# Graph attention on one Trainium2 core: first source terms in blocks of sixteen windows, and first-edge one-hots that are stored once and multiplied in bfloat16 parts

## The chip, the core and the metric

The kernel runs on one core of a Trainium2 chip. TensorE (PE, with PEld for its weight loads), VectorE (DVE), ScalarE (ACT) and GpSimd (POOL) each work through a queue of their own; SyncE (SP) issues most of the transfers, and POOL issues the gathers. The metric is the device time of one execution in microseconds; a lower time is better. Several runs of a kernel are made, and their median is given. One more execution is recorded by the hardware profiler, with its own time.

## The reference, cut to what matters

A graph of N = 6250 nodes with 128 features each and E = 100,000 edges, sorted by their target `dst`, goes through four sublayers, each as `x = x + layer(relu(layernorm(x)))`: a mean of neighbours with two weights, a filter with a product over each node's edges, three mean layers ("SAGE"), and three attention layers. The change concerns the attention layers and what is prepared for them:

```python
def gat_conv(x, src, dst, ea, W, a_src, a_dst, We, a_edge, bias):
    s, d = concat([src, loops]), concat([dst, loops])     # each node also has a loop to itself
    h = x @ W
    al_s, al_d = h @ a_src, h @ a_dst
    al_e = ea_full @ We @ a_edge
    alpha = leaky_relu(al_s[s] + al_d[d] + al_e, 0.2)
    ex = exp(alpha - segment_max(alpha, d)[d])
    coef = ex / (segment_sum(ex, d)[d] + 1e-16)
    return segment_sum(h[s] * coef[:, None], d) + bias
for l in (1, 2, 3):
    h = batch_norm(leaky_relu(gat_conv(h, ...), 0.01))
```

So an edge needs one number of its source (`al_s[s]`, the "source term"), one of its target (`al_d[d]`), and a softmax over all edges of the same target.

## The kernel before, in words

*Tiling.* Nodes lie on P = 125 partitions with T = 50 nodes each. The attention layers treat the nodes in two ways. The *early* nodes, those of the first 64 partitions, are aggregated by matrix products with one-hot matrices. The *late* nodes, 3050 of them as R2 = 122 partitions with T2 = 25 each, are aggregated by gathers and a running sum. The late edges lie as 125 partitions with C2 = 400 edges each, in the order of their targets.

*What is prepared once.* During the first SAGE layer, `late_edges` (L1118) computes for each late node `lt.q` and `lt.c`: the partition and the column of its first edge; `lt.slot` is a row of the numbers 0 to 399. `early_edges` (L1187) stores one-hots of the early edges in DRAM in bfloat16, among them `hot_t` (which source partition an edge has, 128 windows of 128 x 128 for each of GP = 5 groups) and `col` (which of the 50 nodes of that partition). A tile pool in `late_edges` has one buffer for each name (`bufs=1`). The scheduler puts this work among the first products of SAGE layer 0 (L848), whose operands (`piece`, L884) come from DRAM over SP's queue, as the new tiles of this case would.

*A layer* (`attention_split`, L1297) makes h, al_s and al_d with TensorE, stores h with al_s as a table (`gtable`) and al_d (`own_d`), reads al_d of the late nodes back as `late_d` [122, 25] and of the early nodes as `early_d`, and splits al_s into three bfloat16 parts whose sum is al_s (`parts`). Then `split_edges` (L1370) does the edges, and a batch normalization ends the layer. In `split_edges`:

- `source_terms(g, al_s)` (L1376) finds the source terms of one group of early edges. In each of 16 rounds it loads 8 windows of `hot_t` and `col`, does 24 matmuls into `x_ps` (8 windows by three parts, L1387), and on DVE multiplies by `col` (L1391, recorded as the helper's line L73) and sums (L1392).
- `softmax(g, al_s)` (L1395) is the softmax over one group, eight steps, mostly small DVE operations that follow one another.
- `ready(step)` (L1439) loads and builds the one-hots `hot_n` and `hot_c` for one of 160 steps of four windows; `product(unit, m)` (L1459) is the aggregation of a quarter of a group, 50 matmuls (L1464).
- `late()` (L1475) is the late work as a generator: 50 blocks of eight columns with four steps each. A block gathers eight rows for each partition with POOL (L55), computes exponentials and the running sum on DVE, and stores it. Then `late_fix` (L1599, 7 steps) and `late_tail` (L1635, 5 rounds of 8 steps) follow: the latter gathers each late node's last sum, loads its own row of the table (`own_h`, L1642) and finishes it.
- `first_edges()` (L1518) brings al_d to the late edges. For each of 25 columns of late nodes DVE builds a one-hot `run` [122, 125], scaled by `late_d` (L1524), and a one-hot `col_f` [122, 400] (L1525), and TensorE adds their fp32 product to `at_ps` (L1526). The result has al_d at each node's first edge; a scan (L1532) spreads it over the node's other edges, and it is added to `ade`, the edge term of the late edges. The first column comes by a gather instead (L1530).

*The order.* PE, DVE and ACT do their instructions of `split_edges` in the order of the program: a chain of dependencies is laid over them at the end (L1591 to 1597). SP's and POOL's order is the scheduler's. The program's order is this: first `source_terms(0)` with `first_edges` drawn into it, which is the *lead-in's* first part; then `softmax(0)`, with one step of late work after each of its steps; then the *loop* of 160 steps. A loop step does four fp32 matmuls (L1564), prepares step + 2, draws seven matmuls of the last unit's product, evicts to `m` (L1569), and does a part of the next group's source terms and softmax. The late work is drawn by a count: after step s, `10 + 1.3 (s + 1)` of its 200 block steps are to be done (L1577), and from step 149 on three steps of what follows are drawn in each loop step (L1580). What is left of it comes after the last product.

*Names that the change touches.* The buffers `m` (two, 125 x 50 x 160 fp32, one for each unit of eight loop steps) and `hot_n` (three, 128 x 1000 fp32), the PSUM buffers `cnt` (two, 1024 fp32 a partition) and `o` (two; `at_ps` takes one), the SBUF buffers `acc` (two) and `run` (two). A transfer over all 125 partitions goes through `bulk` (L48), which makes two of it, over 112 and 13 partitions.

Of the kernel before, what the change touches and what calls it, by code (L numbers as in the profile page):

```python
# [9 lines left out]
F32 = mybir.dt.float32  # L10
BF16 = mybir.dt.bfloat16
I32 = mybir.dt.int32
AF = mybir.ActivationFunctionType
OP = mybir.AluOpType
AX = mybir.AxisListType
# [4 lines left out]
P = 125  # L20
C = E // P
T = N // P
# [3 lines left out]
NW, NG, WCAP = 5, 10, 128  # L26
# [4 lines left out]
P1, C2 = 64, 400  # L31
N1, E1 = P1 * T, E - P * C2
R2, T2 = 122, 25
# [6 lines left out]
def kernel(ctx: ExitStack, tc: tile.TileContext, a: dict, out: bass.AP):  # L40
    nc = tc.nc

    const = ctx.enter_context(tc.tile_pool(name="const", bufs=1))
    dram = ctx.enter_context(tc.tile_pool(name="dram", bufs=1, space=DRAM))
# [9 lines left out]
    def gather(dst, table, idx):  # L54
        nc.gpsimd.indirect_dma_start(  # L55
            out=dst, out_offset=None, in_=table,
            in_offset=bass.IndirectOffsetOnAxis(ap=idx, axis=0))
# [14 lines left out]
    def tt(o, x, y, op):  # L72
        nc.vector.tensor_tensor(o, x, y, op)  # L73

    def ts(o, x, s1, op0, s2=None, op1=None):
        if op1 is None:
            nc.vector.tensor_scalar(o, x, s1, None, op0=op0)  # L77
        else:
            nc.vector.tensor_scalar(o, x, s1, s2, op0=op0, op1=op1)  # L79

    def stt(o, x, s, y, op0, op1):
        nc.vector.scalar_tensor_tensor(o, x, s, y, op0=op0, op1=op1)  # L82
# [957 lines left out]

    late_hist = dram.tile([P * C2 + 1, W], F32, name="late_hist")

    class Late:


# [72 lines left out]
    def late_edges(lt):  # L1118
        with tc.tile_pool(name="le", bufs=1) as pool, tc.tile_pool(name="le_ps", bufs=1, space=PSUM) as ps:
# [58 lines left out]
            ts(inside[:, 1:2], inside[:, 0:1], -SKIP, OP.mult, SKIP, OP.add)  # L1178
            ts(fse[:, 2:3], fse[:, 1:2], -float(E1), OP.add)
            stt(lt.fix, fse[:, 2:3], inside[:, 0:1], inside[:, 1:2], OP.mult, OP.add)  # L1180

            row_ps = ps.tile([128, P], F32, name="le_row")
            transpose(row_ps, dst_f[:, C2 - 1:C2].to_broadcast([P, 128]))
# [186 lines left out]
    def split_edges(lt, i, table, own_d, bias, parts, early_d, late_d, ade, tails, stats, stats_l, pool, ps):  # L1370
# [144 lines left out]
            yield from late_fix(lt, tails, pool, ps)  # L1515
            yield from late_tail(lt, table, late_d, lt.e_self[i], bias, stats_l, pool, ps)

        def first_edges():  # L1518

            at_ps = ps.tile([P, C2], F32, name="at_ps", tag="o", bufs=2)  # L1520
            for c in range(T2):
                run = pool.tile([R2, P], F32, name="run")
                col = pool.tile([R2, C2], F32, name="col_f")
                ts(run, lt.slot[:R2, :P], lt.q[:, c:c + 1], OP.is_equal, late_d[:, c:c + 1], OP.mult)  # L1524
                ts(col, lt.slot[:R2, :], lt.c[:, c:c + 1], OP.is_equal)  # L1525
                nc.tensor.matmul(at_ps, lhsT=run, rhs=col, start=(c == 0), stop=(c == T2 - 1))  # L1526
                yield
            at_start = pool.tile([P, C2], F32, name="at_start", bufs=1)
            nc.scalar.activation(at_start, at_ps, AF.Copy)
            gather(at_start[:, 0:1], own_d, lt.first)  # L1530
            yield
            nc.vector.tensor_tensor_scan(at_start, lt.same, at_start, 0.0, op0=OP.mult, op1=OP.add)  # L1532
            tt(ade, ade, at_start, OP.add)
            yield

        traced = nc.cur_bb.bb.instructions
        n0 = len(traced)
        steps = GP * 32
        al_s = pool.tile([128, 128], F32, name="al_s")
        edges_late, firsts = late(), first_edges()  # L1540
        for n, _ in enumerate(source_terms(0, al_s)):
            if n >= 4:
                next(firsts, None)
        for _ in firsts:
            pass
        for n, _ in enumerate(softmax(0, al_s)):
            next(edges_late)
        hots = [ready(0)]
        next(edges_late)
# [1 line left out]
        done = n + 2  # L1551
        before, m = iter(()), None
        for step in range(steps):
            g, s = divmod(step, 32)
            unit, u = divmod(step, 8)
            if s == 0 and g < GP - 1:
                al_s = pool.tile([128, 128], F32, name="al_s")
                terms, soft = source_terms(g + 1, al_s), softmax(g + 1, al_s)
            if u == 0:
                m = pool.tile([128, T, NW, 32], F32, name="m")  # L1560
            cnt = ps.tile([128, 4, 256], F32, name="cnt", bufs=2)
            hot_n, hot_c = hots.pop(0)
            for w in range(4):
                nc.tensor.matmul(cnt[:P, w, :T * NW], lhsT=hot_c[:, w, :P], rhs=hot_n[:, w, :], start=True, stop=True)  # L1564
            if step + 2 < steps:
                hots.append(ready(step + 2))
            for _ in islice(before, 7):
                pass
            nc.scalar.activation(m[:P, :, :, u * 4:u * 4 + 4].rearrange("p l k q -> p k l q"),  # L1569
                                 cnt[:P, :, :T * NW].rearrange("p w (k l) -> p k l w", k=NW), AF.Copy)  # L1570
            if g < GP - 1:
                if s < 20:
                    for _ in islice(terms, 2 if s % 5 < 3 else 1):
                        pass
                else:
                    next(soft, None)
            while done < min(200, 10 + (step + 1) * 1.3):  # L1577
                next(edges_late)
                done += 1
            if step > 148:  # L1580
                for _ in islice(edges_late, 3):
                    pass
            if u == 7:
                for _ in before:
                    pass
                before = product(unit, m)
# [410 lines left out]
```

## Time and profile before

| | |
|---|---|
| median of 3 runs | 7281.8 us (7275.46 to 7299.53) |
| profiled execution: its time, its span | 6198.65 us, 6196.9 us |
| mean granted TensorE clock | 0.854 |
| attention layer 0, 1, 2: first source term starts | 3713.16, 4531.79, 5354.40 us |
| their first loop matmul | 3818.95, 4637.62, 5461.27 us |
| their loop step 149 | 4410.8, 5232.8, 6055.7 us |
| their last product's matmuls start | 4476.35, 5299.11, 6121.13 us |
| their batch normalization starts | 4508.87, 5331.48, 6153.65 us |
| SAGE layers, with what is prepared for attention | from about 2190 to 3713 us |

The profiled execution took 1083 us less than the median of the runs. The profile is of that one execution; places in it are given in microseconds from the start of its span. A row of groups names a line, an engine, an operation, its output and inputs with their shapes and the number of such instructions, then their busy time, the mean duration of one in nanoseconds, and the idle time of the engine ahead of them with what ended it. Where a helper records the instruction the line is the helper's: L55 is a gather, L73, L77 and L82 are DVE operations. A row of a table of stretches gives busy time and count for PE, PEld, DVE, ACT and POOL, then the granted TensorE clock, the busy share of the 16 DMA engines and the gigabytes a second that they moved. A row of a timeline gives start, duration, engine, line and operation; "SPq" is SP's queue, and such a row is the issue of a transfer and not its landing.

The largest groups of an attention layer are, by the trace of layer 0 (3713 to 4532 us): the gathers of rows on POOL, 402.5 us in 400; the loop's fp32 matmuls (L1564), 309.1 us in 1280; the product's (L1464), 303.2 us in 2000; ACT's `hot_c` (L1455), 233.9 us in 640; the eviction to `m` (L1569), 157.9 us in 160; DVE's running sum (L82), 141.2 us in 399. The source terms' matmuls (L1387) take 73.2 us in 1921.

### The profile page before, as it was taken

To read this page: it belongs to the slowest core of one execution; us is meant where nothing else is said; L and a number is where in the kernel's file an instruction comes from. 1 tells how busy PE (TensorE), PEld (TensorE's weight loads), DVE (VectorE), ACT (ScalarE), POOL (GpSimd) and SP (SyncE) were. 2 spreads that over 40 slices of the span, in tenths; PEclk is the share of its full clock that TensorE was granted. 3 is DMA by queue.
4 is the path that set the end of the run, shared out by engine and by line. 5 is a ranking of instruction groups with operands and counts; after the bars stand their busy time and mean duration, and the time that the engine had idled before them with its cause. 6 is when DMAs were issued, how large, how long until landed. Compare 5 with 4: busy or idle time off the path is not lost. (4 is left out here: it accounts for less than half of the span.)

```text
span 6196.9 us, 99429 instructions
## 1 busy us (share of the span) xinstructions
PE 5145.0 (83%) x34443; PEld 3914.9 (63%) x34443; DVE 4012.7 (65%) x12892; ACT 3053.7 (49%) x6329; POOL 2222.9 (36%) x2177
## 2 busy tenths in 40 slices
PE   3299996898888579989979986999859998679995
PEld 3267763444444457756657764888738888468885
DVE  7899976999999541156552126777457775477773
ACT  0166657999999310000000012777627667357674
POOL 0100007777776400000000004666326665256661
PEclk9999995655555589989989987999969999789997
DMA  1133336666665146468875534766337665366662
GB/s 42 28 133 136 137 143 178 193 193 200 194 193 177 34 172 229 182 240 298 310 276 211 190 128 141 199 193 183 107 107 206 194 192 140 90 172 193 193 181 82
DMA packets 410722, 1051.98 MB, mean 170 GB/s; under 512 B 83516, under 2 KB 206429, under 8 KB 391909
## 3 DMA queue, kind: packets, MB, share of 16 engines
q1 hardware_dynamic: 334356, 899.22, 43.4%
q0 software_dynamic: 70080, 143.09, 10.1%
q8 instruction: 273, 4.47, 0.3%
q10 hardware_dynamic: 5768, 3.19, 0.2%
q14 instruction: 245, 2.01, 0.1%
HBM read 742.37 MB, written 302.92 MB: 169 GB/s over the span
## 5 line engine op out<-in xcount | busy, mean ns | idle before, releaser
L55 POOL DMA_INDIRECT rows<-gtable,l_src x1200 | 1210.4, 1009 | 1651.2 <-DMA hot_t<-hot_t 1003.5
L848 PEld LDWEIGHTS <-parts 128*128 128x128 bf16 x12000 | 1181.2, 98 | 449.6 <-issue 37.0
L848 PE MATMUL o<-piece,parts 128*128 128x305 bf16 (+1 forms) x9000 | 1249.8, 299 | 23.1 <-DMA piece<-adj 23.1
L1464 PE MATMUL o<-m,hst 125*128 125x160 f32 x6000 | 913.8, 304 | 98.2 <-ACT m L1569 98.2
L1464 PEld LDWEIGHTS o<-m,hst 125*128 125x128 f32 x6000 | 874.9, 193 | 140.9 <-ACT m L1569 121.4
L1564 PE MATMUL cnt<-hot_n,hot_c 128*125 128x250 f32 x3840 | 931.2, 385 | 15.3 <-ACT m L1569 9.8
L55 POOL DMA_INDIRECT rows<-table,src_all x800 | 817.0, 1021 | 256.1 <-issue 210.1
L1564 PEld LDWEIGHTS cnt<-hot_n,hot_c 128*125 128x125 f32 x3840 | 701.2, 191 | 94.0 <-ACT m L1569 13.1
L1455 ACT ACTIVATE hot_c<-hot,coef_t 128x125 f32<-128x125 bf16 x1920 | 701.6, 390 | 0.1
L865 ACT ACTIVATE h_t<-h_ps 128x500 f32<-128x500 f32 x80 | 34.6, 432 | 968.5 <-PE h_ps L863 761.7
L1569 ACT ACTIVATE m<-cnt 125x1000 f32<-125x1000 f32 x480 | 473.8, 987 | 34.1 <-PE cnt L1564 34.0
L816 ACT ACTIVATE adj<-cnt 128x1000 bf16<-128x1000 f32 x320 | 382.8, 1214 | 182.7 <-PE cnt L814 181.1
L661 PE MATMUL z<-w,s 128*125 128x128 f32 x1600 | 369.8, 402 | 113.8 <-DVE s L82 113.5
L848 PE MATMUL o<-adj,parts 128*128 128x320 bf16 (+1 forms) x3000 | 451.8, 297 | 9.4 <-ACT adj L816 8.7
L661 PEld LDWEIGHTS z<-w,s 128*125 128x125 f32 x1600 | 316.4, 293 | 219.9 <-DVE s L82 185.0
L82 DVE SCALAR_TENSOR_TENSOR acc<-acc,ex,rows 125x130 f32<-125x130 f32 x1197 | 423.1, 353 | 34.3
L1454 ACT ACTIVATE hot_n<-half_n 128x250 f32<-128x250 bf16 x960 | 384.0, 400 | 32.9 <-DMA half_n<-node 32.3
L652 PE MATMUL z<-bf,w 128*128 128x500 f32 x400 | 376.4, 1042 | 27.0 <-ACT bf L621 27.0
L850 DVE COPY agg<-o 128x320 f32<-128x320 f32 x80 | 38.5, 482 | 521.6 <-PE o L848 521.6
L73 DVE TENSOR_TENSOR one<-x_ps,col 128x400 f32<-128x400 f32 x240 | 137.3, 572 | 360.0 <-PE x_ps L1387 301.3
L77 DVE TENSOR_SCALAR hot_n<-slots_b,id_t 128x250 bf16<-128x250 bf16 x1250 | 359.9, 288 | 0.0
L77 DVE TENSOR_SCALAR hot_p<-slots_b,hi_t 128x128 bf16<-128x128 bf16 x1250 | 316.7, 253 | 37.3 <-PE cnt L814 37.2
(463 smaller groups left out, 7167.6 us busy)
## 6 DMA issues: line engine op xcount, KB each, us to landing
piece<-adj SPq DMA_DIRECT2D x60, 2000.0 KB
piece<-adj SPq DMA_DIRECT2D x60, 1906.2 KB
late_hist<-acc SPq DMA_DIRECT2D x150, 455.0 KB
hot_t<-hot_t SPq DMA_DIRECT2D x240, 256.0 KB
hot<-hot SPq DMA_DIRECT2D x240, 256.0 KB
half_n<-node SPq DMA_DIRECT2D x480, 125.0 KB
dist<-ew_dram SPq DMA_DIRECT2D x50, 1000.0 KB
ea<-in_edge_attr SPq DMA_DIRECT2D x100, 448.0 KB
```

Source lines behind the costliest of these rows:

```text
L55: nc.gpsimd.indirect_dma_start(out=dst, out_offset=None, in_=table, in_offset=bass.IndirectOffsetOnAxis(ap=idx, axis=0))
L77: nc.vector.tensor_scalar(o, x, s1, None, op0=op0)
L82: nc.vector.scalar_tensor_tensor(o, x, s, y, op0=op0, op1=op1)
L652: nc.tensor.matmul(z1, lhsT=w1, rhs=bf, start=False, stop=True)
L661: nc.tensor.matmul(z2[:, j, :], lhsT=s1[:, j, :], rhs=w2, start=False, stop=j == HB - 1)
L816: nc.scalar.activation(adj[:, :, :, q - q0:q - q0 + n], cnt[:, :n, :T * NW].rearrange("p w (k l) -> p k l w", k=NW), AF.Copy)
L848: yield nc.tensor.matmul(o[:, :n], lhsT=parts[:, l, s, :], rhs=adj(l), start=(l == 0 and s == 0), stop=(l == T - 1 and s == 2))
L1454: nc.scalar.activation(hot_n[:, w, :], half_n[:, w // 2, :], AF.Copy)
L1455: nc.scalar.activation(hot_c[:, w, :P], lt.hot[:, w0 % WB + w, :P], AF.Copy, scale=coef_t[g][:, w0 + w:w0 + w + 1])
L1464: nc.tensor.matmul(o, lhsT=hst[:, l, :D], rhs=m[:P, l, :], start=(l == 0), stop=(l == T - 1))
L1564: nc.tensor.matmul(cnt[:P, w, :T * NW], lhsT=hot_c[:, w, :P], rhs=hot_n[:, w, :], start=True, stop=True)
L1569: nc.scalar.activation(m[:P, :, :, u * 4:u * 4 + 4].rearrange("p l k q -> p k l q"), cnt[:P, :, :T * NW].rearrange("p w (k l) -> p k l w", ...
```

## The change: what it does

There are four parts.

1. *One-hots stored once.* `late_edges` also builds all 25 one-hots of `run` (128 wide, not scaled) and of `col_f` (400 wide) in bfloat16, five columns at a time, and stores them in two DRAM tensors, `run_dram` [122, 3200] and `first_dram` [122, 10000]: 50 DVE operations and ten stores, in all 3.2 MB.
2. *`first_terms` in place of `first_edges` and of `source_terms(0)`.* At a layer's start two transfers bring `hot_t` of group 0, 64 windows each, and two bring `col`, into the two buffers `m`; one brings all of `run`, behind the first half. Five transfers bring the first-edge one-hots, five columns each, into the three `hot_n` buffers. The source terms run as 8 blocks of 16 windows in a `cnt` buffer (48 matmuls, then one multiplication and one sum of 800 elements a partition). `late_d` is split into three bfloat16 parts after block 1. After each of blocks 2 to 6, five columns of first edges are done: ACT scales the stored `run` by each of the three parts (`late_p`), and TensorE adds the three bfloat16 products to `at_ps`. The other groups keep `source_terms` as it is.
3. *Order.* `softmax(0)`'s first three steps are drawn between the parts of `first_terms`, so that five and not eight of them have a late step after them. The gather of the first column goes to a tile of its own, `at_first`, ahead of everything else in `split_edges`.
4. *Pace of the late work.* `10 + 1.45 (s + 1)` in place of `10 + 1.3 (s + 1)`, and three steps of the rest from step 141 on in place of 149.

```diff
+    run_dram = dram.tile([R2, T2 * 128], BF16, name="run1")
+    first_dram = dram.tile([R2, T2 * C2], BF16, name="first1")
+    KC = 5
...
+            for c0 in range(0, T2, KC):
+                runs = pool.tile([R2, KC, 128], BF16, name="le_runs")
+                cols = pool.tile([R2, KC, C2], BF16, name="le_cols")
+                for c in range(KC):
+                    ts(runs[:, c, :], lt.slot[:R2, :128], lt.q[:, c0 + c:c0 + c + 1], OP.is_equal)
+                    ts(cols[:, c, :], lt.slot[:R2, :], lt.c[:, c0 + c:c0 + c + 1], OP.is_equal)
+                nc.sync.dma_start(run_dram[:, c0 * 128:(c0 + KC) * 128], runs.rearrange("p c j -> p (c j)"))
+                nc.sync.dma_start(first_dram[:, c0 * C2:(c0 + KC) * C2], cols.rearrange("p c j -> p (c j)"))
...
-        def first_edges():
...
-            for c in range(T2):
-                run = pool.tile([R2, P], F32, name="run")
-                col = pool.tile([R2, C2], F32, name="col_f")
-                ts(run, lt.slot[:R2, :P], lt.q[:, c:c + 1], OP.is_equal, late_d[:, c:c + 1], OP.mult)
-                ts(col, lt.slot[:R2, :], lt.c[:, c:c + 1], OP.is_equal)
-                nc.tensor.matmul(at_ps, lhsT=run, rhs=col, start=(c == 0), stop=(c == T2 - 1))
-                yield
+        def first_terms(al_s):
+            XB, HW = 16, 64
+            stores = []
+            for h in range(2):
+                m = pool.tile([128, T, NW, 32], F32, name="m").rearrange("p l k q -> p (l k q)").bitcast(BF16)
+                hot_t, col = m[:, :HW * 128], m[:, HW * 128:HW * (128 + T)]
+                nc.sync.dma_start(hot_t, hot_t_dram[0][:, h * HW * 128:(h + 1) * HW * 128])
+                nc.sync.dma_start(col, col_dram[0][:, h * HW * T:(h + 1) * HW * T])
+                stores.append((m, hot_t.rearrange("p (w j) -> p w j", j=128), col.rearrange("p (w l) -> p w l", l=T)))
+                if h == 0:
+                    runs = m[:R2, HW * (128 + T):HW * (128 + T) + T2 * 128]
+                    nc.sync.dma_start(runs, run_dram)
+            cols = []
             at_ps = ps.tile([P, C2], F32, name="at_ps", tag="o", bufs=2)
+            def columns(k):
+                col = pool.tile([128, 4, T * NW], F32, name="hot_n", bufs=3)
+                col = col.rearrange("p w n -> p (w n)").bitcast(BF16)[:R2, :KC * C2]
+                nc.sync.dma_start(col, first_dram[:, k * KC * C2:(k + 1) * KC * C2])
+                return col
...
+            def late_parts():
+                for k in range(3):
+                    nc.vector.tensor_copy(late_b[:, k % 2, :], late_d if k == 0 else late_p[:, 2, :])
+                    nc.vector.tensor_copy(late_p[:, k, :], late_b[:, k % 2, :])
+                    if k < 2:
+                        tt(late_p[:, 2, :], late_d if k == 0 else late_p[:, 2, :], late_b[:, k % 2, :], OP.subtract)
+            def first_edge(c):
+                if c % KC == 0:
+                    cols.append(columns(c // KC))
+                run = pool.tile([R2, 3, 128], BF16, name="run", bufs=3)
+                for k in range(3):
+                    nc.scalar.activation(run[:, k, :P], runs[:, c * 128:c * 128 + P], AF.Copy, scale=late_p[:, k, c:c + 1])
+                for k in range(3):
+                    nc.tensor.matmul(at_ps, lhsT=run[:, k, :P], rhs=cols[-1][:, c % KC * C2:(c % KC + 1) * C2],
+                                     start=(c == 0 and k == 0), stop=(c == T2 - 1 and k == 2))
+            c = 0
+            for b in range(8):
+                _, hot_t, col = stores[b // 4]
+                w0 = b % 4 * XB
+                x = ps.tile([128, 4, 256], F32, name="cnt", bufs=2).rearrange("p a b -> p (a b)").rearrange(
+                    "p (h n) -> p h n", h=2)[:, :, :8 * T].rearrange("p h (w l) -> p h w l", l=T)
+                for w in range(XB):
+                    for k in range(3):
+                        nc.tensor.matmul(x[:, w // 8, w % 8, :], lhsT=hot_t[:, w0 + w, :], rhs=parts[:, k, :],
+                                         start=(k == 0), stop=(k == 2))
+                one = pool.tile([128, 2, 8, T], F32, name="acc")
+                tt(one, x, col[:, w0:w0 + XB, :].rearrange("p (h w) l -> p h w l", h=2), OP.mult)
+                nc.vector.tensor_reduce(al_s[:, b * XB:(b + 1) * XB].rearrange("p (h w) -> p h w", h=2), one, AX.X, OP.add)
+                if b == 1:
+                    late_parts()
+                while 2 <= b and c < min(T2, (b - 1) * 5):
+                    first_edge(c)
+                    c += 1
+                if b == 5:
+                    yield
             at_start = pool.tile([P, C2], F32, name="at_start", bufs=1)
-            nc.scalar.activation(at_start, at_ps, AF.Copy)
-            gather(at_start[:, 0:1], own_d, lt.first)
+            nc.scalar.activation(at_start[:, 1:], at_ps[:, 1:], AF.Copy)
+            nc.scalar.activation(at_start[:, 0:1], at_first, AF.Copy)
             yield
             nc.vector.tensor_tensor_scan(at_start, lt.same, at_start, 0.0, op0=OP.mult, op1=OP.add)
             tt(ade, ade, at_start, OP.add)
...
-        edges_late, firsts = late(), first_edges()
-        for n, _ in enumerate(source_terms(0, al_s)):
-            if n >= 4:
-                next(firsts, None)
-        for _ in firsts:
-            pass
-        for n, _ in enumerate(softmax(0, al_s)):
+        at_first = pool.tile([P, 1], F32, name="at_first", bufs=1)
+        gather(at_first, own_d, lt.first)
+        edges_late, soft = late(), softmax(0, al_s)
+        terms = first_terms(al_s)
+        next(terms)
+        next(soft)
+        next(terms)
+        next(soft)
+        next(soft)
+        next(terms, None)
+        for n, _ in enumerate(soft):
             next(edges_late)
...
-            while done < min(200, 10 + (step + 1) * 1.3):
+            while done < min(200, 10 + (step + 1) * 1.45):
...
-            if step > 148:
+            if step > 140:
```

## The prediction

> **What bounds the kernel now.** I read the page first, then the busy time by stretch of attention layer 0, the groups of its first stretch, the timelines of three places, and the DMA queues of one short window.
>
> ```profile
> PE 5145.0 (83%) x34443; PEld 3914.9 (63%) x34443; DVE 4012.7 (65%) x12892; ACT 3053.7 (49%) x6329; POOL 2222.9 (36%) x2177
> PEclk9999995655555589989989987999969999789997
> ```
>
> TensorE has the largest share, but that is an average. The change lies in the three attention layers (3713 to 6155 us), so each is cut where its work changes. Columns: stretch, length, busy time of PE, PEld, DVE, ACT, POOL, granted clock, DMA share, GB/s.
>
> ```profile
> 3713.10:3797.60 84.50, 51.49 (x434) 30.04 (x434) 35.60 (x89) 1.79 (x2) 24.16 (x25) 0.61 0.38 109
> 3797.60:3819.00 21.40, 0.99 (x3) 0.41 (x3) 19.96 (x62) 1.84 (x8) 9.16 (x9) 0.50 0.24 64
> 3819.00:4410.80 591.80, 554.60 (x4499) 512.97 (x4500) 435.40 (x1287) 431.07 (x1192) 370.43 (x368) 0.98 0.68 192
> 4410.80:4476.30 65.50, 44.06 (x246) 38.57 (x244) 22.15 (x95) 38.71 (x102) 22.94 (x24) 0.90 0.24 64
> 4476.30:4508.90 32.60, 17.64 (x110) 15.29 (x110) 12.83 (x55) 9.45 (x24) 3.49 (x4) 0.74 0.05 10
> ```
>
> In order: first source terms with first edges; first softmax; the loop to step 149; the loop with the late tail; the last product and the rest of the late tail. No engine is full in the first stretch, and the clock is 0.61. The second is DVE's. The third is TensorE's. The lead-in, from the first source term to the loop's first matmul, takes 105.8, 105.8 and 106.9 us in the three layers. Its largest groups:
>
> ```profile
> L1526 PE MATMUL at_ps<-col_f,run 122*125 122x400 f32 x50 | 38.5, 871 | 22.5 <-DVE col_f L77 22.5
> L1387 PE MATMUL x_ps<-als_parts,hot_t 128*128 128x50 bf16 x384 | 19.9, 209 | 6.6 <-DMA hot_t<-hot_t 3.6 <-DVE one L73 1.3 <-DMA gtable<-hst 1.1
> L73 DVE TENSOR_TENSOR one<-x_ps,col 128x400 f32<-128x400 f32 x16 | 9.2, 575 | 42.9 <-PE x_ps L1387 39.2 <-issue 3.7
> ```
>
> PE and DVE wait for each other in turn: this is what the blocks of 16 and the stored one-hots take away. The line that decides, I think, is elsewhere. own_h (L1642) is the only sizeable load in the kernel over 122 partitions in one DMA; a window in which it runs alone:
>
> ```profile
> DMA packets 84, 0.22 MB, mean 44 GB/s; under 512 B 0, under 2 KB 0, under 8 KB 84
> q1 hardware_dynamic: 84, 0.22, 12.8%
> ```
>
> 12.8% of 16 engines is two engines, at 44 GB/s, where 2 MB piece loads show 311 GB/s (2700 to 3100 us).
>
> **What the skill says.** "DMA: Bandwidth & Descriptors", section "Why a DMA increments its semaphore by 16 and not by 1": a transfer takes the largest number of engines, up to 16, that divides the slowest dimension on both sides, always the lowest-numbered ones; 122 has no such divisor but 2. The trace agrees (12.8%). The same page, "Queues, rings and completion order": each engine takes a queue's descriptors in order, so a transfer on all 16 waits behind one that sits on two. No run here shows that yet. "TensorE: Matmul & The Clock Gate", Part 1: the clock halves after idle windows; the trace agrees (0.50 to 0.61 in the lead-in, 0.98 in the loop).
>
> **The change, part by part.**
>
> *Loads of the lead-in.* Per layer SP now issues, after the ald stores: col (0.8 MB), late_d, early_d, runs (122 rows of 6,400 B), the second hot_t (2.1 MB), col, and three of five first-edge blocks (122 rows of 4,000 B), the last two as hot_n buffers come free. Only the first hot_t goes ahead of the table stores. An own_h row of 2,600 B costs two engines 2600/22 = 118 ns. [...]4,000 B cost about 0.17 us and 6,400 B 0.26 us. Each engine then has 61 x 0.26 = 15.6 us for runs, 5 x 61 x 0.17 = 51 us for first edges, 5 for hot_t, 2 for col, 3.5 for of, hot, half_n and the next hot_t, and about 7 for the late gathers of the same time: 84 us. SP reached this place at 3719 (late_d issued 3717.8), so the last block lands near 3720.5 + 84 + 1.5 = 3806. The other bound is a spread over 16 engines: 6.6 MB at about 220 GB/s (311 less the gathers), landing near 3745. I take the first, since own_h shows it.
>
> *Work of the lead-in.* TensorE: 384 source matmuls stay; 50 fp32 passes of 871 ns (43 us) become 75 bf16 matmuls of 400 columns. L848 does 305 of 320 columns in 42.51 us, 139 ns each, so 174 ns at full and 348 at half clock: 13 to 26 us. ScalarE: 75 scalings at about 0.29 us from start to start (two hot_c in 0.68 us), 22 us, under the loads. DVE loses 50 one-hot operations (19 us) and 16 pairs of 0.57, gains 8 pairs of about 1.05 (800 elements) and eight small ops. All of it hides under the wait for the last block. What does not: the last five edges at half clock, 15 x 0.348 = 5.2 us; block 7, which is queued behind them on PE, 48 x 59 ns = 2.8; its DVE pair 2.4; the softmax rest. That was 21.4 us with eight late steps; with five it is about 17 (softmax from the transpose 8.4, scan and add 1.6, late 6.3, hand-overs). First loop matmul: 3806 + 5.2 + 2.8 + 2.4 + 17 = 3833.4 against 3819.0: **+14 us a layer**. Were the loads spread, ScalarE would set the end (3740 + 25 x 0.9, then 4.5 + 17 + 3 for the cold clock): 3789, -30.
>
> *Loop.* POOL's gathers take 1.02 + 0.30 = 1.32 us, a block of eight 10.6; at 1.45 steps of late work a step of 4.0 us asks for a block every 4/1.45 x 4.0 = 11.0. It fits with 4% to spare. The count restarts at 6 instead of 9, so step 0 issues six late steps, not three: 3 x 1.33 = 4 us of DVE ahead of the one-hots that PE waits for, and the gather of block 3 starts only when block 0 is used. I take +7 a layer; bounds 2 (covered by PE's own 1.9 us batches) and 15 (each of the first six blocks late by 2 us more). The gather moved to the head of POOL waits for ald and holds the row gathers behind it about 2 us, under the lead-in.
>
> *End of a layer.* Late work ends at step 131, its 47 tail steps run in steps 141 to 156, nothing is left for the end. Before:
>
> ```profile
> 4476.35 13.85 PE L1464 MATMUL o<-m,hst 125*128 125x160 f32 x100 [2.00 <-ACT m L1569]
> 4507.64 1.04 DVE L1680 BATCH_NORM_STATS2 stats_l<-z_l 128x6 f32<-128x122 f32 x5
> 4508.87 0.70 DVE L1342 BATCH_NORM_AGGREGATE bn_mv<-stats 128x2 f32<-128x120 f32 x1 [0.19 <-issue]
> ```
>
> From the product's end (4490.2) to the statistics 18.7 us of tail go, 1.5 stay. Fourteen tail steps move into the loop: the 33 there cost 63.2 - 11 x 3.6 = 23.6 us of stall, about 10 of it one gather's latency, so 14 more cost about 5. **-12 a layer**; bounds -7 and -17.
>
> *Stores, once.* 50 one-hots (about 0.29 and 0.43 us, 18 us of DVE) and ten stores of 122 rows are put among the first SAGE products, where PE was full:
>
> ```profile
> 2212.16 42.51 PE L848 MATMUL o<-piece,parts 128*128 128x320 bf16 x305
> 2234.41 0.34 SPq L884 DMA_DIRECT2D piece<-adj  x1
> 2254.04 0.48 DVE L850 COPY agg<-o 128x305 f32<-128x305 f32 x1
> ```
>
> A block of five takes its two engines 61 x (0.068 + 0.17) = 14.5 us, its buffers are single, and the compiled DVE order puts blocks 1, 2 and half of 3 ahead of the second agg copy, and block 3's rest ahead of the next PSUM reads. Walked through: store 0 lands 2247, store 1 2266, run 2 2275, agg copy 2277 instead of 2254, store 2 2285, node terms done 2292 instead of 2261. The piece loads of the same SP queue land meanwhile. **+30**; bounds 10 (stores on 16 engines) and 45 (a piece late as well).
>
> *Sum.* 30 + 3 x (14 + 7 - 12) = **+57 us**. The profiled execution took 6198.65 us (span 6196.9), and would take 6256. The median of the runs is 7281.8, 17% longer; no profile shows why. Most of these terms are DMA and DVE waits, so I add them unscaled: **7339 us**.
>
> **Rivals.** *Loads and stores spread or drain in time* (the other side): for it, the loads are few and large; against it, own_h. From where the last block lands before about 3780 the lead-in is shorter. -30 + 7 - 12 = -35 a layer, +10 once: 7187. *Even*: the store is covered (+15), the loop costs 2 and the end gives 17: 15 + 3 x (14 + 2 - 17) = +12, 7294; for it, the 26 us of stall in the tail stretch that a better spread could take too. *POOL becomes the bound*: a gather of 1.5 us gives 376 x 1.5 = 564 us against 131 steps x 4.03 = 528, +36 a layer, 7447; against it, gathers in the busy loop show 1.25 to 1.36.
>
> **Numbers.** Forecast 0.62, spread 0.13, even 0.18, POOL 0.07. Within 0.3% (22 us, about what can be told from no change) lie the even case and little else: slower 0.70, same 0.17, faster 0.13. The forecast's bounds (10 to 45 once; 5 to 20, 2 to 15 and -17 to -7 a layer) and the even case give 7270 to 7405; the spread and POOL cases, 0.20, stay outside.
>
> **What would show it.** In the profile after: the first-edge blocks at 12 to 13% of 16 engines for some 50 us of each lead-in; at_ps matmuls waiting for DMA hot_n<-first in groups of 15; PE's clock at 0.5 there; a lead-in of 115 to 125 us; no tail after the last product; a hole in PE near 2255 to 2290. A lead-in under 95 us, or these loads at over 100 GB/s, proves the forecast wrong.

## The result, and the profile after

The changed kernel takes 7385.3 us (median of 4 runs, 7366.8 to 7393.1) against 7278.6 us of the kernel before (4 runs, 7267.6 to 7299.5): a ratio of 1.0139, 95% interval 1.0108 to 1.0171, so about 101 us slower. The forecast was 7339 us, 57 us slower.

The chips differ: on some the kernel before takes 7255 to 7300 us, on another 6185 us, and the profile shown ahead (6199 us) is like the latter; so stages are compared below with a second profile of the kernel before, of 7272 us. The ratio of an experiment is taken against runs of the kernel before on its own chip; where two ratios are subtracted, both come from chips of the slower kind.

Two rows of the page of the changed kernel (span 7391.3 us): busy time, and the granted clock by slice.

```profile
PE 5408.3 (73%) x34518; PEld 4092.0 (55%) x34518; DVE 3984.9 (54%) x12768; ACT 3133.4 (42%) x6557; POOL 2177.9 (29%) x2177
PEclk9999955555555589899899688889688888688888
```

Layer 0 in stretches, with the columns as before the prediction: first source terms with first edges, first softmax, the loop to `late_fix`, the loop from there to its last step, and the rest up to the batch normalization. First the kernel before, in its second profile:

```profile
4049.00:4157.30 108.30, 52.66 (x434) 30.82 (x434) 35.43 (x89) 1.79 (x2) 23.94 (x25) 0.57 0.29 84
4157.30:4178.60 21.30, 0.95 (x2) 0.36 (x2) 19.86 (x62) 1.76 (x8) 9.09 (x9) 0.50 0.23 65
4178.60:4987.60 809.00, 640.25 (x4498) 562.97 (x4499) 433.61 (x1286) 433.88 (x1192) 367.50 (x368) 0.88 0.48 140
4987.60:5053.40 65.80, 44.86 (x244) 39.17 (x243) 21.55 (x94) 36.80 (x98) 21.52 (x22) 0.87 0.22 63
5053.40:5090.30 36.90, 20.09 (x115) 17.47 (x113) 13.44 (x56) 11.06 (x27) 4.86 (x5) 0.73 0.04 10
```

Then the changed kernel:

```profile
4084.40:4184.70 100.30, 34.96 (x459) 27.32 (x459) 19.65 (x34) 25.85 (x78) 23.90 (x25) 0.66 0.37 113
4184.70:4202.10 17.40, 0.82 (x3) 0.34 (x3) 16.15 (x48) 1.59 (x7) 3.08 (x4) 0.58 0.17 46
4202.10:5039.10 837.00, 627.63 (x4335) 544.90 (x4336) 435.00 (x1280) 412.35 (x1135) 368.65 (x373) 0.86 0.47 134
5039.10:5140.20 101.10, 75.79 (x418) 66.89 (x417) 38.67 (x163) 66.78 (x178) 26.65 (x27) 0.90 0.22 62
5140.20:5159.80 19.60, 16.12 (x104) 15.62 (x102) 1.34 (x5) 2.35 (x5) 0.00 (x0) 0.91 0.00 1
```

The lead-in is 118 us in place of 130, the last stretch 20 in place of 37: both are gains. The loss is in the third and fourth rows. In the third, 809 us held 149 loop steps (5.43 us each) and 837 us now hold 141 (5.94 us each), while TensorE was busy for less of it. All three layers and the setup, by the same places in the two traces:

| stretch | before, again | after | change | forecast |
|---|---|---|---|---|
| SAGE products, with the setup among them | 1447.7 | 1480.5 | +33 | +30 |
| lead-ins, three layers | 390.2 | 357.1 | -33 | +42 |
| loop, first to last step, three layers | 2628.7 | 2801.6 | +173 | +36 |
| last step to batch normalization, three layers | 113.0 | 58.8 | -54 | -51 |
| the rest of the span | 2690.7 | 2693.4 | +3 | 0 |
| span | 7270.2 | 7391.3 | +121 | +57 |

(The forecast's -12 for a layer's end was -17 of tail gone and +5 of stall in the loop; the table puts the 5 with the loop's 7.)

The forecast named marks to look for. The first-edge matmuls of layer 0, grouped as in the prediction, wait for loads, and for nothing else:

```profile
L1571 PE MATMUL at_ps<-hot_n,run 122*125 122x400 bf16 x75 | 23.4, 497 | 58.1 <-DMA hot_n<-first 58.1
```

The loads are on two engines. DMA queues of 9 us in which little but a first-edge block runs:

```profile
DMA packets 122, 0.47 MB, mean 52 GB/s; under 512 B 6, under 2 KB 6, under 8 KB 122
q1 hardware_dynamic: 116, 0.46, 12.5%
```

12.5% of 16 engines is two, at 52 GB/s. SP's issue of the first three blocks takes 38.2 us in all (from 4091.4 us on; in the split kernel below their six transfers are issued within 4.7 us), so whatever SP issues next is late too. And the late tail is gone from a layer's end: the last product's matmuls start at 5142.90, take 15.53 us, and the statistics follow at 5159.77, 1.3 us after them.

### The profile page after: what moved, and what is told of

Read it like the earlier page. It is cut to its first block, busy times and chain, and to the rows that moved or that the text cites. A ratio compares the mean times of both kernels' runs of the same rounds, so it can differ in the third digit from the quotient of the medians.

```text
span 7391.3 us, 99580 instructions
## 1 busy us (share of the span) xinstructions
PE 5408.3 (73%) x34518; PEld 4092.0 (55%) x34518; DVE 3984.9 (54%) x12768; ACT 3133.4 (42%) x6557; POOL 2177.9 (29%) x2177
## 4 chain that ended last, share of the span: by engine, by line
PE 30%; DVE 10%; DMA 9%; issue 7%; ACT 5%; another core or an unknown queue 4%; SPq 1%; POOL 1%; DVEq 0%; ACTq 0%; POOLq 0%
PE o L848 11%; PE o L1477 7%; PE cnt L1633 6%; DVE acc L82 2%; DMA hot_n<-first 2%; ACT hot_c L1468 2%; PE x_ps L1400 2%; DMA ee_rows<-part 2%; DMA hot<-ee_hot 1%; ACT m L1638 1%; SPq L1551 1%; DMA half_n<-node 1%; DMA first<-le_cols 1%; ACT hot_n L1467 1%
## 5 line engine op out<-in xcount | busy, mean ns | idle before, releaser
L55 POOL DMA_INDIRECT rows<-gtable,l_src x1200 | 1189.2, 991 | 2511.1 <-DMA late_d<-ald 1045.3
L1477 PE MATMUL o<-m,hst 125*128 125x160 f32 x6000 | 1021.4, 319 | 269.9 <-issue 194.5
L1633 PE MATMUL cnt<-hot_n,hot_c 128*125 128x250 f32 x3840 | 1079.2, 425 | 100.9 <-issue 69.4
L1477 PEld LDWEIGHTS o<-m,hst 125*128 125x128 f32 x6000 | 952.2, 205 | 356.8 <-issue 242.7
L55 POOL DMA_INDIRECT rows<-table,src_all x800 | 792.6, 991 | 599.3 <-DVE run L79 332.4
L1633 PEld LDWEIGHTS cnt<-hot_n,hot_c 128*125 128x125 f32 x3840 | 783.7, 214 | 231.8 <-issue 96.9
L73 DVE TENSOR_TENSOR one<-x_ps,col 128x400 f32<-128x400 f32 x192 | 109.8, 572 | 724.9 <-remote 446.6
L77 DVE TENSOR_SCALAR hot_n<-l_slot,l_id_t 128x250 f32<-128x250 f32 x960 | 295.1, 350 | 223.2 <-remote 123.0
L621 ACT ACTIVATE soft<-z 128x500 f32<-128x500 f32 (+1 forms) x400 | 231.2, 578 | 405.4 <-remote 282.4
L1400 PE MATMUL x_ps<-als_parts,hot_t 128*128 128x50 bf16 x4608 | 200.9, 192 | 254.8 <-issue 188.4
```

Of the source, the lines that this page charges most:

```text
L55: nc.gpsimd.indirect_dma_start(out=dst, out_offset=None, in_=table, in_offset=bass.IndirectOffsetOnAxis(ap=idx, axis=0))
L1400: nc.tensor.matmul(x[:, w, :], lhsT=hot_t[:, w, :], rhs=parts[:, k, :], start=(k == 0), stop=(k == 2))
L1477: nc.tensor.matmul(o, lhsT=hst[:, l, :D], rhs=m[:P, l, :], start=(l == 0), stop=(l == T - 1))
```

## The experiments

### A second profile of the kernel before

The kernel is unchanged.

> The kernel before, once more, for a profile of an execution that takes as long as its timed runs: about 7280 us by every theory. What is asked is where its stages lie: the lead-in of an attention layer (first source term to first loop matmul) should again take about 106 us, 12 less than the 117.7 us of the changed kernel's layer 0; the loop and the setup, which take longer here than in the profile of 6199 us, give the base for the rest of the 107 us.

Measured: 7272.1 us. The lead-in was not 106 us but 129.6, 130.0 and 130.6 us in the three layers; that is read from TensorE's waits in layer 0's first stretch (who waited for what: us in all, times, longest):

```profile
PE at_ps L1526 <- DVE col_f L77: 42.7, 11, 24.1
```

In the profile ahead the same row had 22.5 us in 13 waits, the longest 1.9. One wait of 24.1 us accounts for the difference of 23.8 us in the lead-in; the two other layers have one of 24.1 and one of 22.7 us. POOL's first 24 gathers of the layer run from 4053.5 to 4083.2 us. The timeline across that wait, POOL's gathers left out:

```profile
4064.55 0.70 PE L1387 MATMUL x_ps<-als_parts,hot_t 128*128 128x50 bf16 x12
...
4087.48 0.32 SPq L1381 DMA_DIRECT2D hot_t<-hot_t  x1
4087.48 0.57 DVE L73 TENSOR_TENSOR one<-x_ps,col 128x400 f32<-128x400 f32 x1 [25.89 <-remote]
```

From 4065.3 to 4087.5 us TensorE, DVE and SP do nothing. The last matmuls ahead of SP's and DVE's next instructions had ended by the record at 4065.3; SP and DVE go on at the same moment, some 4 us after the last gather. On this chip something seems to hold the hand-over between engines while POOL issues gathers (the runs without gathers, below, bear on that). The base from which the forecast's +14 was counted was thus 24 us too small for the timed runs.

### The stores alone

```diff
 (the kernel before, with the change to late_edges and the two DRAM tensors; nothing reads them)
```

> The kernel before with one part of the change: the one-hots are built and stored in the first SAGE layer, and nobody reads them. Forecast's theory (DVE and the PSUM evictions wait for stores on two engines): +30 us over before, 7309 (10 to 45). Rival, the stores drain beside the products: within 5 us of before, 7284. Rival, the setup is where the forecast's missing 50 us lie: +80 us, 7360.

Measured: 7309.0 us against 7255.3, ratio 1.0067 (1.0045 to 1.0088), so 49 us slower (33 to 64). The SAGE products, with the setup among them, take 1482.6 us, 35 more than in the second profile of before. The forecast's step is right in sign and size: 35 us in the trace and 49 in the runs, for 30 (10 to 45).

### All transfers of 122 rows made as 112 and 10

```diff
+    def rows122(dst, src):
+        nc.sync.dma_start(dst[0:PS], src[0:PS])      # PS = 112
+        nc.sync.dma_start(dst[PS:R2], src[PS:R2])
...
-                    nc.sync.dma_start(runs, run_dram)
+                    rows122(runs, run_dram)
 (and so for the first-edge blocks and the ten stores)
```

> The changed kernel with each transfer of 122 rows made as two, of 112 and of 10 rows, for the stores and for the loads. Forecast's theory (a transfer of 122 rows sits on two DMA engines, and the last first-edge block sets the lead-in): the blocks land some 40 us sooner, ScalarE's scalings become the bound, the lead-in shrinks from 118 to about 88 us, and the setup by 20 us: 7385 - 3 x 30 - 20 = 7275 us. Rival, the transfers are slow by their size or their place in the queue: the blocks land as before and the time stays at 7370 to 7385 us.

Measured: 7221.5 us against 7255.3, ratio 0.9931 (0.9904 to 0.9958). The changed kernel's ratio was 1.0139, so the split is worth about 2.1%, some 150 us. The lead-in is 82.1, 82.2 and 82.4 us, 37 less than with two engines, and the SAGE products 1436.7 us, 44 less; the expectation had 30 and 20. Layer 0's first stretch in the split kernel, and its first-edge matmuls:

```profile
4036.10:4100.90 64.80, 29.70 (x460) 22.58 (x460) 19.70 (x34) 24.03 (x78) 23.89 (x25) 0.71 0.59 175
```

```profile
L1576 PE MATMUL at_ps<-hot_n,run 122*125 122x400 bf16 x75 | 18.4, 389 | 27.5 <-ACT run L1574 14.6 <-DMA hot_n<-first 12.9
```

DMA's share is 0.59 in place of 0.37, the wait for blocks 12.9 us in place of 58.1. The forecast's theory of the lead-in and of the stores stands. (The SAGE products are even 11 us shorter than in the kernel before, which has none of the new work; what else moved there isn't shown.) What replaces the load wait is one wait of 14.6 us for ScalarE's `run`, which ends at 4077.4 us, some 5 us after the last of the first 24 gathers (4041.4 to 4072.6 us).

### Only the loads split

```diff
 (the split kernel, with the ten stores as one transfer of 122 rows each, as in the changed kernel)
```

> The changed kernel with only the loads of 122 rows split; the stores in setup stay on two engines. The setup of the split kernel is 44 us shorter than the changed kernel's in the traces, so this should give those back: 7221 + 44 = 7265 us, and SAGE products that end some 33 us later, in proportion to their start, than those of the kernel before. Rival, the stall in setup is DVE's 50 one-hot operations and not their stores: the time stays near 7221 us.

Measured: 7264.7 us against 7260.1, ratio 1.0005 (0.9988 to 1.0021): 0.74% over the split kernel, 54 us. The lead-ins stay at 81.5 to 82.3 us, and the SAGE products take 1483.8 us, as in the other kernels with stores on two engines (1478.4 to 1482.6). So it is the stores and not the 50 one-hot operations, which the split kernel has too, that stall the setup. TensorE's waits in the first 170 us of the setup, first in the changed kernel, then in the split one:

```profile
PE y_ps L871 <- DVE agg L850: 33.1, 2, 18.5
PE y_ps L870 <- DVE y_nodes L82: 6.2, 1, 6.2
```

```profile
PE y_ps L870 <- DVE y_nodes L82: 5.0, 2, 2.8
PE y_ps L871 <- DVE agg L850: 1.4, 1, 1.4
```

The wait of 18.5 us is the second `agg` copy. It starts 60.5 us after the first product, in the second profile of before 41.1 us: 19 us late, where the forecast had 23.

### The old pace

```diff
-            while done < min(200, 10 + (step + 1) * 1.45):
+            while done < min(200, 10 + (step + 1) * 1.3):
...
-            if step > 140:
+            if step > 148:
```

> The changed kernel with the pace of the late work as before (1.3 a step; the rest from step 149 on). Forecast's theory: the pace costs 7 us in a layer's loop and gives 12 back at its end, so undoing it costs 3 x 5 = 15 us: 7400 us. Rival, the faster pace is where the forecast's missing 50 us lie: 7335 us. Rival, the work is the same wherever it is put: 7385 us.

Measured: 7296.5 us against 7255.3, ratio 1.0044 (1.0023 to 1.0066). Against the changed kernel's 1.0139 that is 0.95%, some 69 us less. The rival is right: the pace costs, even more than the missing 50 us, since the lead-in gave some time back. The lead-ins (117.9, 120.0, 118.7 us) are those of the changed kernel; loop and end together take 2761.3 us in the three layers, 99 less than in its trace (2860.5).

How this comes about is seen in the late work's gathers. They are those of layer 0 after the loop's start, each row with the durations in ns and the first and last start in us; first the second profile of before, then the changed kernel:

```profile
L55 POOL DMA_INDIRECT rows<-gtable,l_src x368: 942/947/2000, 4178.1 to 4950.6; - x184
```

```profile
L55 POOL DMA_INDIRECT rows<-gtable,l_src x373: 938/944/2012, 4202.0 to 4978.9; - x187
```

They take 772.5 us at the pace of 1.3 and 776.9 us at 1.45: a block of eight every 16.8 and 16.7 us, though POOL's own work on one gather is 0.94 us, with 0.30 us between two. A pace of 1.45 asks for a block every 2.76 steps: 16.7 / 2.76 = 6.05 us a step (measured 5.94). A pace of 1.3 asks for one every 3.08: 16.8 / 3.08 = 5.45 (5.43). So on this kind of chip the late work isn't finished sooner by a faster pace. It lies beside fewer steps, and more steps are left after it. This sum describes the trace and doesn't say what holds a block at 16.7 us: in the changed kernel POOL waited 244 us of that time for row buffers to come free, so its own work doesn't fill it.

### The pace alone

The kernel before with the opposite of that edit.

> The kernel before with one part of the change, the pace of 1.45 and the rest of the late work from step 141 on. Theory (the gathers of a layer need some 775 us beside the loop at either pace, and the steps that are left after them run at their own rate): the loop and its end grow by 25 to 30 us a layer, as they do in the split kernel, so 60 to 90 us: 7320 to 7350 us. Rival, the pace costs only together with the new lead-in, whose count starts at 6 and not at 9: 7265 to 7280 us.

Measured: 6210.4 us against 6185.2, ratio 1.0038 (1.0024 to 1.0051), 24 us slower, on the chip where before takes 6185 us. The sign is as expected, the size is not: three layers' loops and ends grow by 26 us, 9 a layer. There a loop step to `late_fix` takes 582.7 / 141 = 4.13 us in place of 591.8 / 149 = 3.97. The pace costs without the new lead-in, so the rival falls; how much depends on the chip. The gathers of layer 0's loop take 523 us here and 561 in the profile of 6199 us, so on such a chip a faster pace does finish them sooner.

### The gathers left out, at both paces

```diff
-                for j in range(NB):
-                    gather(all_rows[:, j, :], table, lt.src[:, c0 + j:c0 + j + 1])
+                nc.gpsimd.memset(all_rows.rearrange("p c f -> p (c f)"), 0.0)
```

> The split kernel with the 400 gathers of late rows of each layer left out: one memset of a block's rows on POOL takes the place of eight gathers, so the late sums are of zeros; everything else stays, at the pace of 1.45. Theory: between the loop's start and the last gather some 775 us pass at either pace, because TensorE's stalls lie beside the gathers; without them a step takes about 3.8 to 4.1 us, and a loop 620 to 660 us in place of 930: about 6350 us. Rival, DVE's and ScalarE's part of the late work holds the loop: the loop stays above 800 us, 6900 us or more.

> The same without the gathers of late rows, at the old pace (1.3; rest from step 149 on). Theory (the faster pace costs because the gathers come to lie beside fewer steps, whose rate they set, while the steps after them run no faster than TensorE can): without gathers the two paces lie within 15 us of each other in a layer's loop and end. Rival, the pace costs by what DVE is given ahead of the loop's one-hots: the old pace is still 20 us a layer better, as it is with the gathers.

Measured: 6428.3 us at the pace of 1.45 and 6423.1 us at 1.3, one run each, on a chip where before takes 7260 us. Loop and end together take 705.6, 710.2 and 705.3 us in the three layers at 1.45, and 701.2, 699.3 and 701.3 us at 1.3: 4 to 11 us apart, where the split kernels with gathers are 27, 20 and 14 us apart. The theory holds: 240 us of each layer, and most of what the pace costs on such a chip (some 14 of 20 us a layer), come with the gathers. The rest of the cost doesn't. Layer 0's loop to `late_fix`, 141 steps at 1.45 and 149 at 1.3:

```profile
4086.40:4670.00 583.60, 533.29 (x4335) 491.77 (x4335) 452.15 (x1279) 408.86 (x1135) 46.79 (x46) 0.97 0.50 150
4103.00:4700.70 597.70, 558.30 (x4499) 516.31 (x4500) 459.06 (x1297) 430.85 (x1193) 47.03 (x46) 0.97 0.50 149
```

That is 4.14 us a step against 4.01, without a gather. From first to last step the loops take 686.0, 690.6 and 685.7 us at 1.45 against 663.9, 663.6 and 662.8: 22 to 27 us longer, of which the end of the layer gives 16 to 19 back.

### The gathers replaced by plain transfers

```diff
-                for j in range(NB):
-                    gather(all_rows[:, j, :], table, lt.src[:, c0 + j:c0 + j + 1])
-                rows = all_rows[:P]
+                rows = all_rows[:P]
+                bulk(rows.rearrange("p c f -> p (c f)"), nodes(table, c0 % 40, NB, W), nc.gpsimd)
```

> The split kernel at the pace of 1.45 with the 400 gathers of late rows of each layer replaced by plain transfers of as many bytes from the same table, two for each block of eight columns, issued by POOL as the gathers are; the late sums are of other nodes' rows. If it is the gathers' issuing on POOL, or their addressing, that slows TensorE in the loop: a loop as without gathers, 690 us, and about 6450 us in all. If it is their bytes on the DMA engines (0.53 MB a block): the loop stays above 850 us, 7000 to 7200 us.

> Plain transfers in place of the late rows' gathers once more, at the pace of 1.45: the last time on record of it came from a chip on which the kernel before takes 6185 us, and where gathers cost the loop little. On a chip where before takes some 7260 us: a loop (to its last step's products) of 690 us and 6430 us in all if it is the gathers' issuing or addressing that holds TensorE there; above 850 us, and 7000 us or more, if it is the bytes. On a chip where before takes 6190 us: 6115 us, as before, and nothing new.

Measured: first 6114.5 us, on the chip where before takes 6185 us. Layer 0's loop to `late_fix` on that chip at the pace of 1.45, with gathers (the pace alone, above) and with plain transfers:

```profile
3810.10:4392.80 582.70, 533.62 (x4335) 492.77 (x4336) 433.28 (x1269) 407.59 (x1134) 369.29 (x368) 0.97 0.66 192
3766.20:4354.00 587.80, 536.75 (x4335) 495.12 (x4336) 428.93 (x1280) 410.50 (x1135) 48.63 (x92) 0.96 0.67 190
```

So there the gathers cost the loop nothing that shows, and they aren't what makes its steps longer at the faster pace (4.13 us with them, 4.17 without). The same kernel again, where before takes 7299.6 us: 6464.7 us, ratio 0.886 (0.883 to 0.889). Layer 0's loop to `late_fix` there:

```profile
4118.00:4703.90 585.90, 535.47 (x4334) 494.40 (x4335) 428.57 (x1279) 410.87 (x1135) 48.64 (x92) 0.97 0.68 191
```

585.9 us in place of 837 (832 in the split kernel), with a DMA share of 0.68 where both have 0.47, and POOL's queue moved 24.21 MB where it moved 24.95 in the split kernel's loop: it isn't the bytes. The lead-ins are shorter too, 68 to 70 us in place of the split kernel's 82, and layer 0's is without that kernel's wait of 14.6 us for ScalarE. TensorE's waits over the same stretch, first in the changed kernel (its four largest), then with plain transfers:

```profile
PE x_ps L1400 <- issue: 66.3, 68, 9.0
PE o L1477 <- issue: 62.0, 68, 3.5
PE o L1477 <- ACT m L1638: 25.9, 11, 10.6
PE cnt L1633 <- issue: 25.2, 36, 1.7
```

```profile
PE o L1482 <- ACT m L1642: 38.0, 17, 4.9
PE x_ps L1405 <- DVE one L73: 7.3, 3, 6.5
PE cnt L1637 <- ACT m L1642: 4.8, 7, 1.9
```

"issue" is time in which TensorE waited for nothing that the profile shows: 153 us of it in the changed kernel (172 waits), none with plain transfers, none without gathers, and none in the profile of 6199 us, which has the gathers. So it takes both, the gathers and such a chip. The granted clock is 0.86 in the changed kernel's loop and 0.97 here, on a chip of the same kind, so these chips aren't slow by their clock alone. Eight indirect transfers a block became two plain ones, so the runs don't tell whether it is the addresses, the number of transfers or POOL's time for them (368.65 us against 48.64 in the stretch).

### Better versions

The split kernel with the old pace:

```diff
 (the edits of the split kernel and of the old pace together)
```

> The changed kernel with every 122-row transfer made as 112 and 10 rows, and with the pace of the late work as before (1.3; rest from step 149 on). If the two costs are independent, as the theory now has it (two-engine transfers in setup and lead-in; pace in the loop), the 60 us that the old pace gave to the changed kernel come off the split kernel's 7221: 7160 us, 1.3% under before. Rival, the two are one cost (a late start that the pace makes up for, or the other way round): 7200 to 7220 us.

Measured: 7149.6 us against 7260.1, ratio 0.9839 (0.9817 to 0.9860): 1.6% faster than before. The two gains add up, as expected (0.9931 less the pace's 0.0095 is 0.9836). The lead-ins are 82 us, the SAGE products 1432.5 us.

And with a slower pace than before's:

```diff
-            while done < min(200, 10 + (step + 1) * 1.45):
+            while done < min(200, 10 + (step + 1) * 1.25):
...
-            if step > 140:
+            if step > 151:
```

> The split kernel at a slower pace than before's, 1.25 a step, and the rest from step 152 on. Theory: the time to the last gather stays near 775 us, six more steps lie beside it, 4 us each come off the loop's end, and nine more tail steps come after the loop for 5 to 10 us: 10 to 15 us a layer less than at 1.3, about 7115 us. Rival, at 1.3 the gathers no longer set the rate: 7150 to 7175 us.

Measured: 6063.5 us against 6185.2, ratio 0.9805 (0.9792 to 0.9819), on the chip of 6185 us. Loop and end together take 690.4, 693.5 and 693.5 us there, and in the profile of 6199 us, at 1.3, 689.9, 693.9 and 692.4: this pace gave nothing on such a chip, so the rival holds there. The gain is that of the split kernel, lead-ins of 68.1, 66.3 and 67.2 us in place of 106. Whether 1.25 is better than 1.3 on the slower chips stays open; both versions beat the kernel before.

## Why the prediction was right, and where it was not

The time, 7385 us, lies in the range (7270 to 7405), the direction is right, and the size is 101 to 107 us where 57 were forecast. But the terms were not all right: two errors of opposite sign hide in the sum. By the traces the lead-ins are 75 us under their term and the loop 137 us over it. That the total still lies in the range is luck.

*Loads of the lead-in: right.* "The last block lands near 3806" is 92.8 us after the first source term; in layer 0 the last block's matmuls start at 4176.9, 92.5 us after 4084.4. The lead-in was to be 105.8 + 14 = 119.8 us, and is 117.7, 120.5 and 118.9. The split shows the cause: 37 us less. That it fits to 0.3 us is chance: at 52 GB/s on two engines a row of 4,000 B takes 0.154 us and not 0.17, which is 5 us less for five blocks, while the last two blocks follow after 12.3 and 11.7 us and not, as those before them, after 9.6.

*The lead-in as a difference: wrong sign.* The first step that failed is "Most of these terms are DMA and DVE waits, so I add them unscaled". The base of 106 us comes from the profile of 6199 us; in the timed runs it is 130, since TensorE, DVE and SP stand still for 22 us beside the first 24 gathers. In the changed kernel the gathers lie under the wait for the loads, and by the fit above seem to cost nothing more. So each lead-in gave 11 us and did not cost 14.

*Setup: right.* +33 us in the traces, +49 in the runs with the stores alone, for +30. "The compiled DVE order puts blocks 1, 2 and half of 3 ahead of the second agg copy" is what the waits show, and the split stores take the cost away.

*Loop: right sign, size wrong.* The second step that failed is the loop's term: +7 a layer, with 5 of stall from the tail, by "It fits with 4% to spare". The traces have +58. The runs divide that. About 24 us a layer belong to the pace with no slowing by gathers: 22 to 27 us in the runs without them, and 24 for the pace alone on the chip of 6185 us, where 12 were forecast and 20 was the bound. The fit of POOL's gathers doesn't matter for these: steps at 1.45 are as long with plain transfers (4.17 us, on that chip) or with neither (4.14, on a slower one) as with gathers there (4.13). Which of the steps' added late work holds TensorE isn't shown. Undoing the pace takes 50 of the 58 back (loops of 885.1, 891.0 and 875.0 us), so a further 26 come with it on the slower chips alone, beside gathers (8 aren't assigned). There a block takes 16.7 us and not the 10.6 of POOL's own work, and steps get longer as the pace gets faster; what slows TensorE beside the gathers stays open.

*End of a layer: right.* -18 us where -17 were forecast before the stall.

*Rivals.* "Spread" is excluded by the 12.5% share; what it describes is the split kernel, whose lead-in of 82 us is near the 76 us that this rival gave (106 - 30). "POOL becomes the bound" had almost the size that the loop shows (+36 against +40 a layer, loop and end together), but by another cause: a gather still took 0.94 us with 0.30 between, not 1.5, and POOL itself waited 244 us for row buffers in layer 0's loop. The range, 7270 to 7405, is a little narrower than the bounds as listed, which add up to 7262 and 7411.

## What to carry to other kernels

Look at how many rows a transfer has before its bytes: 122 rows in one transfer moved at 52 GB/s on two engines, and the same rows as 112 and 10 took 37 us off each of three lead-ins and 44 us off the setup. When a profiled execution is much shorter than the timed runs, its waits are not the base for a difference: first ask which stage holds the gap. A faster pace for background work isn't free: here it made the loops 24 us longer a layer even where gathers slowed nothing, and an end 16 to 19 us shorter was all that it gave. Where the work takes as long at either pace, as the gathers did on the slower chips, a faster pace only moves steps from beside it to behind it.

## What the runs showed of the hardware that was not expected

Chips differ by 17% on this kernel (39 runs of the kernel before on three chips lie between 7230 and 7321 us, nine on a fourth between 6178 and 6191 us), and the difference lies in the stages with gathers: the SAGE products, which have ten gathers in all, take 1449.5 us in the profile of 6199 us and 1447.7 us in that of 7272 us, while layer 0's loop from its first to its last step takes 654.6 and 874.7 us. The first 800 row gathers of the program, ahead of the SAGE products, take 1060 and 1366 us. With the late rows' gathers left out or replaced by plain transfers, a loop takes 686 to 691 us at the pace of 1.45 on the chips of 7260 and 7300 us, and 683 to 688 us (plain) on that of 6185 us. On the slower chips TensorE shows 123 us of "issue" waits in layer 0's loop to `late_fix` (before, 148 waits) and hand-overs between engines seem to come late while POOL issues gathers. What holds them isn't shown by the profile and stays open; so does what sets these chips apart.
